# A four-layer convolution sequence on one core: layer 0 in two strips, layers 1 and 2 as sixteen tiles, and a new model of the order

## The chip, the core and the metric

The kernel runs on one core of one Trainium2 chip. TensorE (PE in the profile), VectorE (DVE), ScalarE (ACT), GpSimd (POOL) and the DMA queue of SyncE (SP) each run their own instruction stream in order and wait for each other by semaphores. PEld is TensorE's loading of weights. The metric is the device time of one execution in microseconds (us); the median of the kernel before is 5206.15 us over three runs (5203.51 to 5209.27). The profile is one further execution.

## The reference

A batch of 32 images of 56 x 56 positions and 96 channels, float32, passes through four layers. Cut to what is computed:

```python
# layer 0: router, expert mix, 1x1 up to 384, 3x3 depthwise, 1x1 down to 96, shortcut
pooled = jnp.mean(x, axis=(1, 2))
rw = jax.nn.sigmoid(pooled @ Wr + br)
Wk = jnp.einsum('be,ecm->bcm', rw, Wpw)
h = jnp.einsum('bhwc,bcm->bhwm', x, Wk) + (rw @ bpw)[:, None, None, :]
h = jax.nn.relu(_bn(h, g1, b1, m1, v1))
h = _cond_dw(h, Wdw, bdw, rw)              # 3x3 depthwise, mixed of 4 experts by rw
h = jax.nn.relu(_bn(h, g2, b2, m2, v2))
Wk2 = jnp.einsum('be,emf->bmf', rw, Wpwl)
h = jnp.einsum('bhwm,bmf->bhwf', h, Wk2) + (rw @ bpwl)[:, None, None, :]
x = _bn(h, g3, b3, m3, v3) + shortcut
# layer 1: x + 5x5 depthwise convolution
# layer 2: relu, 3x3 depthwise, 1x1 (96 to 96), batch norm
# layer 3: shifted window attention (7x7 windows, 3 heads) and an MLP (96, 384, 96), both with
#          layer norm and a residual
```

## The kernel before, in words

The image lies with its channels on the partitions (`xT`, 96 x 3136). Four stages work on four images at a time, one step apart (the loop at L1507): the router of layer 0 (`stage_router`), the rest of layer 0 (`stage_conditional`), layers 1 and 2 (`stage_depthwise`), and layer 3 (`stage_swin`).

**Layer 0.** `stage_conditional` takes the image in `NSTRIP` = 4 strips of `STRIP` = 14 rows, and in each of them `NB` = 3 blocks of 128 of the 384 channels. `expand` makes a block's rows, with a margin row above and below, by two matmuls `banks<-xT,wmix` and two ScalarE activations into `h1`. The nine taps of the 3x3 filter follow: the first on ScalarE (`h<-h,mix`), the other eight on VectorE (`h<-h,mix,h`, 784 elements). `relu` is on ScalarE. `project` brings a strip's 384 channels back to 96, by three matmuls `banks<-h,wmix` for each 7 rows; ScalarE scales and shifts the result into `y`, and GpSimd adds it to `xT` (`add`).

**Layers 1 and 2.** `stage_depthwise` does the 5x5 and the 3x3 depthwise filter on TensorE with banded weights. 8 channels x 4 rows (`RB`) are the 32 rows of a tile, 14 blocks of rows and 56 columns the moving side. `x1` is filled from `xT` by 12 DMAs (`x<-xT`, 32 x 14 x 56). A set is 12 products of 32 x 32 that run beside each other (`together`), one for each of 3 groups and 4 quarters; a filter of n columns needs 2n sets, as a band reaches into the next block of rows. Layer 1 has two halves of 10 sets with 392 columns, layer 2 two parts of 6 sets with 392 and 448. In the trace a product is two records. ScalarE evicts (`x<-banks`), DMAs bring the result back to rows (`filtered<-x`, 36 an image), and the matmuls `banks<-pw,filtered` do the 1x1 product.

**Layer 3.** Its residual rows `res` carry the mean in an extra column. In `perceptron` GpSimd first adds that column (`tb<-res`), then the bias (`tb<-tb,L_conv_b`), and VectorE adds the sum from the banks (`tb<-banks,tb`); a DMA writes `out`.

**What sets the order.** Every instruction is recorded with a target (`PLAN`, `interleave`) by `Recorder`, which then plays a model of the engines (`order`): whatever is ready on an engine and has its buffers starts, the earliest target first. The model's prices are `cost`, `COST`, `LANDING` (of a DMA), `CROSSING` and `TO_TENSOR` (from one engine's end to another's start), and `SHARING` (GpSimd and VectorE slow each other). Where TensorE has nothing for `SPARE_AFTER`, a spare matmul `banks<-ident` of 128 columns is put in. The instructions are then issued in the order found (`give`, L490, whose L500 is therefore the line of nearly every row of the profile). On the chip each engine keeps that order, and waits when an operand is late.

The lines that carry the steps of the change:

```python
    ("sync", "dma_start"): (550, 0),
...
            if e == "gpsimd" or e == "vector" and w.calls[0][0] == "scalar_tensor_tensor":
...
            y = chip.new(ys)
            chip.scalar.activation(y, pt[:C, :RT], AF.Identity, bias=bias3, scale=s3)
...
            chip.gpsimd.tensor_tensor(rows, y, rows, ALU.add)
```

Of the kernel before, what the change touches and what calls it, by code (L numbers as in the profile page):

```python
# [38 lines left out]
RB = 4  # L39
NBLK = H // RB  # L40
STRIP = 14
# [46 lines left out]
def banded(k, before, back):  # L88

    w = np.zeros((NQ, 8, RB, NG, 2, k.shape[2], 8, RB), np.float32)
    for q in range(NQ):
        for g in range(NG):
            first = 32 * g + 8 * ((q - g) % NQ if back else q)
            for m in range(2):
                for row in range(RB):
                    for r in range(RB):
                        dy = RB * m + row - r - before  # L100
                        if 0 <= dy < k.shape[1]:
                            for c in range(8):
                                w[q, c, row, g, m, :, c, r] = k[first + c, dy]
    return w.reshape(P, NG, 2 * k.shape[2], 32)
# [3 lines left out]
def tile_scores_in_range(ctx: ExitStack, tc: tile.TileContext, a: dict, flag: bass.AP):  # L108
# [38 lines left out]
    ("vector", "scalar_tensor_tensor"): (150, 1.16), ("vector", "tensor_tensor"): (180, 0.96),  # L147
    ("vector", "tensor_scalar"): (190, 0.78), ("vector", "tensor_reduce"): (180, 0.95),
    ("vector", "tensor_copy"): (180, 1.1), ("vector", "reciprocal"): (180, 6.2),
    ("scalar", "activation"): (200, 0.72), ("scalar", "copy"): (200, 0.72),  # L150
    ("gpsimd", "tensor_tensor"): (200, 2.1), ("gpsimd", "memset"): (150, 0),
    ("sync", "dma_start"): (550, 0),
}
LANDING = 3000
IMAGE_LANDING = 12000

PLAN = {"router": (-0.14, 1), "conditional": (0.72, 1.14), "depthwise": (1.48, 1.13), "swin": (3.09, 0.92)}
CROSSING = 350

TO_TENSOR = {"vector": 1500, "gpsimd": 1500, "scalar": 1000, "sync": 700}  # L160
SPARE_AFTER = 250
SHARING = 1.36


def cost(engine, method, args, kw):
    if method == "preload_act_table_set":
        return 1300
    out = kw["out"] if "out" in kw else args[0]
    n = math.prod(out.shape[1:])
    if engine == "tensor":  # L170
        if method == "transpose":
            return 127
        k, m = args[1].shape[0], math.prod(args[1].shape[1:])
        if k == 32 and m == 32:
            return 68 * n / 392
        if k == 32:
            return 86
        if m == 32:
            return 75 if n < 128 else 255
        return 195 if n < 128 else 80 + 1.6 * n  # L180
    if len(args) > 3 and args[3] == ALU.pow:
        return 200 + 200 * n
    fixed, each = COST[engine, method]
    if engine == "scalar":
        if kw.get("accum_out") is not None:
            fixed += 190
        if hasattr(kw.get("scale"), "shape"):
            each += 0.37 if hasattr(kw.get("bias"), "shape") else 0.23
        elif hasattr(kw.get("bias"), "shape"):
            each += 0.25  # L190
    return fixed + each * n
# [69 lines left out]
class Recorder:  # L261
# [77 lines left out]
    def order(self):  # L339
# [15 lines left out]
        for w in self.work:  # L355
            for b in w.uses:
                b.left = len(b.users)
        queues = {e: [] for e in self.ENGINES}
# [7 lines left out]
        def available(w):  # L366
            need = {}
# [6 lines left out]

        running = {}

        def share(now):

            nonlocal count
            rate = SHARING if len(running) > 1 else 1.0  # L380
            for r in running.values():
                r["left"] -= (now - r["since"]) / r["rate"]
                r["since"], r["rate"] = now, rate
                r["end"] = free[r["work"].engine] = now + max(r["left"], 0.0) * rate
                heapq.heappush(events, (r["end"], count, r))
                count += 1
# [19 lines left out]
        def begin(w):  # L406
# [9 lines left out]
            if e == "gpsimd" or e == "vector" and w.calls[0][0] == "scalar_tensor_tensor":  # L416
                running[e] = {"work": w, "left": w.ns, "since": now, "rate": 1.0}
                share(now)
                return
            free[e] = now + w.ns  # L420
            heapq.heappush(events, (free[e], count, None))
            heapq.heappush(events, (free[e] + w.landing, count + 1, w))
# [8 lines left out]
        while left:  # L431
            for e in self.ENGINES:
                if free[e] > now:
                    continue
                held = []
                while queues[e]:
                    item = heapq.heappop(queues[e])
                    w = self.work[item[1]]
                    if not available(w):
                        held.append(item)  # L440
                        continue
                    begin(w)
                    left -= 1
                    if e == "tensor":
                        spares, begun = 0, True
                    break
                else:
                    if e == "tensor" and begun and self.spare and now >= free[e] + SPARE_AFTER and self.spare[2].free:
# [5 lines left out]
                        w.ns = cost(e, "matmul", operands, {})  # L454
# [10 lines left out]
            while events and events[0][0] <= now:  # L465
                _, _, w = heapq.heappop(events)
                if isinstance(w, tuple):
                    put(w[0])
                elif isinstance(w, dict):

                    if w["end"] == now and running.get(w["work"].engine) is w:
                        del running[w["work"].engine]
                        w["work"].end = now
                        done(w["work"], now)
                        share(now)
                elif w is not None:
                    done(w, now)
# [26 lines left out]
def kernel(  # L504
# [17 lines left out]
    xTs = ring("xT", [C, H * W], 2)  # L522
    h2s = ring("h2", [P, NB, STRIP * W], 2)
    wmixs = ring("wmix", [C, M], 2)
    wmix2s = ring("wmix2", [P, NB * C], 2)
    ys = ring("y", [C, RT], 2)
# [9 lines left out]
    x3s = ring("x3", [P, NG, NBLK // 2 + 1, W], 1)  # L536
    oTs = ring("oT", [C + 1, 2 * RT], 2)
    x1s = ring("x1", [P, NG, NBLK + 1, W + 4], 1)
    x2s = ring("x2", [P, NG, NBLK + 2, W + 2], 1)
    filtereds = ring("filtered", [C + 1, H, W], 1)  # L540
    h1s = [ring(f"h1{k}", [P, STRIP + 2, W + 2], 1) for k in range(NB)]
    if general:
        ss = ring("scores", [PK, NP, PK], 6)
        pTs = ring("pT", [PK, RT], 4)
# [3 lines left out]
    nc.sync.dma_start(out=xTs.tiles[0], in_=x[0])  # L548


    rooms = [h2s.tiles[0].rearrange("p k n -> p (k n)"), x3s.tiles[0].rearrange("p g m w -> p (g m w)")]
# [94 lines left out]

    held = []
# [13 lines left out]
    band5 = later([P, NG, 10, 32], layouts["k5"], "band5")  # L661
    centre = hold(scratch(P, 64, 1).rearrange("p (n c) -> p n c", n=2), layouts["centre"])
    band3 = later([P, NG, 6, 32], layouts["k3"], "band3")
# [34 lines left out]
    def first_others():  # L698
# [9 lines left out]
        for t in x1s.tiles + x2s.tiles:  # L708
# [17 lines left out]
    def last_others():  # L726
        for g in range(NG):
            for n in range(2):
                at = 5 * n + 2
                nc.vector.tensor_tensor(band5[:, g, at], band5[:, g, at], centre[:, n], ALU.add)  # L730
# [15 lines left out]
    for h1 in h1s:  # L746
        nc.gpsimd.memset(h1.tiles[0], 0.0)
# [15 lines left out]
    def stage_router(b):  # L763

        xT = chip.new(xTs).part(*range(NROW))
# [14 lines left out]
        pooled_w = new_small("pooled_w", [C, P], 1)  # L780
# [21 lines left out]
        prod = new_small("prod", [P, NB * NM, E], 1)  # L802
# [19 lines left out]
        mixed[b] = xT, wmix, wmix2, mix, bias1, biasd, bias3  # L822
        yield 1

    def stage_conditional(b):

        xT, wmix, wmix2, mix, bias1, biasd, bias3 = mixed.pop(b)
        h1s_of = {}

        def expand(strip, k):  # L830

            h1s_of[strip, k] = chip.new(h1s[k]).part(0, 1)

            if strip in (0, NSTRIP - 1):
                chip.gpsimd.memset(h1s_of[strip, k][:, 0 if strip == 0 else STRIP + 1], 0.0)
# [3 lines left out]
            for half, n in enumerate(((last - first + 1) // 2, (last - first) // 2)):  # L839
# [9 lines left out]
                    h1s_of[strip, k][:, at : at + n, 1 : W + 1].part(half),  # L849
# [9 lines left out]
        def project(n, h2):  # L859

            pt = chip.new(mm)
            with chip.together():
                for q in range(NB):
# [3 lines left out]
                        h2[:, q, n % 2 * RT : (n % 2 + 1) * RT],  # L867
# [3 lines left out]
            y = chip.new(ys)  # L871
            chip.scalar.activation(y, pt[:C, :RT], AF.Identity, bias=bias3, scale=s3)
            return y

        def add(n, y):
            rows = xT[:, 7 * n * W : 7 * (n + 1) * W].part(n)
            chip.gpsimd.tensor_tensor(rows, y, rows, ALU.add)

        def projections(strip, h2):
            for n in (2 * strip, 2 * strip + 1):  # L880
# [11 lines left out]
        def relu(h2, k):  # L892
            part = h2[:, k].part(k)
            chip.scalar.activation(part, part, AF.Relu, bias=biasd[:, k : k + 1], scale=s2[:, k : k + 1])

        behind = iter(())
        filtered_before = None
        for at, (strip, k) in enumerate(blocks):
            if k == 0:
                h2 = chip.new(h2s).part(*range(NB))  # L900
            ahead = expand(*blocks[at + 1]) if at + 1 < len(blocks) else iter(())
            h1 = h1s_of[strip, k]
            acc = h2[:, k].part(k).rearrange("p (r w) -> p r w", w=W)
            for t in range(9):
# [7 lines left out]
                yield 1  # L912
                if t in (0, 3):
                    next(ahead, None)
                    yield 1
                if t == 4 and filtered_before:
                    relu(*filtered_before)
                if t in (6, 8):
                    next(behind, None)
                    yield 1  # L920
            filtered_before = h2, k
            if k == NB - 1:
                for _ in behind:
                    yield 1
                behind = projections(strip, h2)
# [5 lines left out]
        added[b] = xT  # L931

    def stage_depthwise(b, res):
# [3 lines left out]
        def lines(t):  # L937

            return t.rearrange("(c r) m w -> c r m w", r=RB)

        x1 = chip.new(x1s)
        x2 = chip.new(x2s).part(0, 1)
# [624 lines left out]
```

## Time and profile before

| | |
|---|---|
| median of three runs | 5206.15 us |
| span of the profiled execution | 5212.6 us |
| granted TensorE clock, mean | 0.985 |
| instructions in the profile | 139630 |
| DMA packets, share of 16 engines | 481940, 14.8% |
| HBM read, written | 41.60 MB, 38.54 MB |
| VectorE taps `h<-h,mix,h` | 3072, mean 1113 ns |
| GpSimd `xT<-y,xT` | 256, mean 1838 ns |
| `tb<-res`, `tb<-tb,L_conv_b` on GpSimd | 256 and 256 |
| DMAs `x<-xT`, `filtered<-x` | 384, 1152 |

A row of the profile's groups has the line, the engine, the operation, what is written from what is read, the shape, how often, the busy time, the mean of one in ns, and the idle time of the engine just before such instructions with what ended it. A row of the timeline has the start, the length and the instructions merged into it. A row of the windows has the stretch, its length, the busy time and number of instructions of PE, PEld, DVE, ACT and POOL, then the granted clock, the DMA engines' share and GB/s.

### The profile page before, as it was taken

The numbers are of one execution on the slowest core, as the hardware profiler recorded it, in microseconds if no ns is written. First come the engines' busy times: TensorE is split into PE (matmuls) and PEld (weight loads), VectorE is DVE, ScalarE is ACT, GpSimd is POOL, SyncE is SP. The second block draws the span as 40 slices with busy tenths as digits, with TensorE's granted clock in tenths as the row PEclk, the third lists the DMA queues.
The fourth block names the chain that finished last, engine by engine and source line by source line (L and its number), as shares of the span: only waits on it lengthen the run. The fifth ranks groups of instructions, "written<-read, shape, count | busy, mean of one in ns | idle before, by whom it ended". The sixth has DMA issues, their size and how long they took to land.

```text
span 5212.6 us, 139630 instructions
## 1 busy us (share of the span) xinstructions
PE 5050.6 (97%) x58578; PEld 3343.9 (64%) x58578; DVE 4300.9 (83%) x5561; ACT 3836.9 (74%) x7649; POOL 3028.8 (58%) x2432
## 2 busy tenths in 40 slices
PE   5789999999999999999999999999999999999999
PEld 4556666666666666666666666666666666666677
DVE  7877988888888888888888888888888888888722
ACT  3457778877778777777877777877777877777755
POOL 5455766565665556666555665656576555566533
PEclk9899999999999999999999999999999999999999
DMA  1111101111111111111111111111111111110110
GB/s 43 23 28 37 38 18 32 33 39 36 39 21 30 31 39 36 39 23 30 33 35 37 37 30 26 30 36 38 37 35 22 32 33 39 36 39 21 23 28 19
DMA packets 482577, 166.34 MB, mean 32 GB/s; under 512 B 477951, under 2 KB 478612, under 8 KB 478868
## 3 DMA queue, kind: packets, MB, share of 16 engines
q1 hardware_dynamic: 481940, 157.33, 14.8%
q8 instruction: 463, 7.59, 0.6%
q14 instruction: 174, 1.43, 0.1%
HBM read 41.60 MB, written 38.54 MB: 15 GB/s over the span
## 4 chain that ended last, share of the span: by engine, by line
PE 74%; POOL 10%; DVE 5%; ACT 5%; issue 4%; DMA 1%; SPq 0%; ACTq 0%; DVEq 0%; POOLq 0%
PE banks L500 74%; DVE h L500 3%; POOL tb L500 3%; POOL lnd L500 2%; POOL xT L500 2%; ACT exps L500 2%; POOL exps L500 2%; POOL var L500 1%; ACT hid L500 1%; ACT h L500 1%; DMA out<-tb 1%; DVE wmix L500 1%; DVE hid L500 1%; ACT slots L500 0%; DVE res L500 0%
## 5 line engine op out<-in xcount | busy, mean ns | idle before, releaser
L500 DVE SCALAR_TENSOR_TENSOR h<-h,mix,h 128x784 f32<-128x784 f32 x3072 | 3309.6, 1113 | 71.1 <-ACT h L500 54.0
L500 POOL TENSOR_TENSOR var<-var,mhalf 112x4 f32<-112x4 f32 (+1 forms) x512 | 775.2, 1519 | 426.3 <-DVE var L500 419.6
L500 PE MATMUL banks<-x,band 32*32 32x392 f32 x24576 | 856.3, 510 | 0.0
L500 POOL TENSOR_TENSOR xT<-y,xT 96x392 f32<-96x392 f32 x256 | 470.2, 1838 | 445.5 <-ACT y L500 444.1
L500 PE MATMUL banks<-xT,wmix 96*128 96x448 f32 (+1 forms) x1536 | 697.9, 553 | 0.5 <-DVE wmix L500 0.5
L500 ACT ACTIVATE h<-h,biasd,s 128x784 f32<-128x784 f32 x384 | 398.9, 1039 | 366.1 <-DVE h L500 366.0
L500 ACT ACTIVATE hid<-banks,c 128x448 f32<-128x448 f32 (+1 forms) x768 | 436.5, 582 | 288.3 <-PE banks L500 279.9
L500 POOL TENSOR_TENSOR tb<-res 112x384 f32<-112x384 f32 (+1 forms) x256 | 476.4, 1866 | 286.7 <-DMA out<-tb 196.7
L500 PEld LDWEIGHTS banks<-w,hid 128*112 128x112 f32 x5376 | 584.7, 183 | 82.0 <-issue 37.8
L500 PE MATMUL banks<-hT,w 96*128 96x448 f32 (+1 forms) x1536 | 615.6, 502 | 0.2 <-DVE tb L500 0.2
L500 POOL TENSOR_TENSOR lnd<-res,var 112x384 f32<-112x384 f32 (+1 forms) x512 | 594.8, 1168 | 32.8 <-PE banks L500 16.2
L500 ACT ACTIVATE h<-banks,bias,s 128x448 f32<-128x448 f32 (+1 forms) x768 | 538.6, 709 | 91.0 <-PE banks L500 85.4
L500 PE MATMUL banks<-w,hid 128*112 128x96 f32 x5376 | 593.1, 267 | 7.4 <-ACT hid L500 6.4
L500 PE MATMUL banks<-h,wmix 128*96 128x392 f32 x1536 | 557.7, 501 | 15.7 <-ACT h L500 15.7
L500 PEld LDWEIGHTS banks<-x,band 32*32 32x32 f32 x24576 | 404.7, 103 | 250.9 <-issue 165.9
L500 ACT ACTIVATE exps<-banks 49x196 f32<-49x196 f32 x1536 | 506.2, 330 | 40.2 <-PE banks L500 15.3
L500 POOL TENSOR_TENSOR exps<-exps,keep_column 49x147 f32<-49x147 f32 x224 | 207.1, 925 | 480.8 <-ACT exps L500 427.4
L500 PEld LDWEIGHTS banks<-h,wmix 128*96 128x96 f32 x1536 | 244.1, 165 | 256.8 <-issue 209.2
L500 PEld LDWEIGHTS banks<-xT,wmix 96*128 96x128 f32 x1536 | 261.2, 192 | 200.7 <-issue 95.5
L500 DVE TENSOR_REDUCE var<-lnsq 112x4 f32<-112x388 f32 (+1 forms) x512 | 253.1, 497 | 157.6 <-POOL lnd L500 118.1
L500 ACT ACTIVATE h<-h,mix 128x784 f32<-128x784 f32 x384 | 364.5, 949 | 18.0 <-POOL h L500 10.1
L500 PEld LDWEIGHTS banks<-hT,w 96*128 96x128 f32 x1536 | 256.4, 190 | 144.9 <-issue 74.8
(132 smaller groups left out, 7460.2 us busy)
## 6 DMA issues: line engine op xcount, KB each, us to landing
xT<-in_x SPq DMA_DIRECT2D x32, 1176.0 KB
x<-xT SPq DMA_DIRECT2D x384, 98.0 KB
out<-tb SPq DMA_DIRECT2D x128, 168.0 KB
filtered<-x SPq DMA_DIRECT2D x384, 49.0 KB
filtered<-x SPq DMA_DIRECT2D x384, 42.0 KB
out<-tb SPq DMA_DIRECT2D x128, 126.0 KB
filtered<-x SPq DMA_DIRECT2D x384, 7.0 KB
wpw<-in_L_conv_Wpw SPq DMA_DIRECT2D x1, 576.0 KB
```

The source lines that it names most:

```text
L500: getattr(getattr(self.nc, w.engine), method)(*args, **kw)
```

## The change

Layer 0 goes in two strips of 28 rows: a tap is 1568 elements, a block needs four `expand` matmuls, and the three blocks share two `h1` buffers and four `h2` buffers. The scale of the last batch norm goes into the weights `wpwl` once at the start; what is left of `y` is one VectorE instruction that adds the bank, `bias3` and `xT`. Layers 1 and 2 take 2 channels x 16 rows as a tile's 32 rows, of which 10 come out of both filters; six such pieces cover the 56 rows. A set has 16 products of 336 columns, and no band reaches over. An image is three parts (`NSET`) of 32 channels: for each 16 DMAs bring `x1` from `xT`, two DMAs from `nought` put zeros where the image ends, 11 DMAs go to `filtered`. The first filter of a part is one block of 80 products, the second one of 48. The MLP's extra column is added by VectorE, in one instruction for each 96 columns. The model gets new prices, prices TensorE by tiling, [...]and picks TensorE work of the tiling in use where targets are close.

```diff
-RB = 4
-NBLK = H // RB
-STRIP = 14
+NSET = 3
+NSLOT = NSET * NQ
+BIN, BMID, BOUT = 16, 12, 10
+NBLK = -(-H // BOUT)
+STRIP = 28
...
-    ("sync", "dma_start"): (550, 0),
+    ("sync", "dma_start"): (120, 0),
 }
+AHEAD = {"vector": 77, "scalar": 100, "gpsimd": 37, "tensor": 0, "sync": 0}
 LANDING = 3000
 IMAGE_LANDING = 12000
-PLAN = {"router": (-0.14, 1), "conditional": (0.72, 1.14), "depthwise": (1.48, 1.13), "swin": (3.09, 0.92)}
-CROSSING = 350
-TO_TENSOR = {"vector": 1500, "gpsimd": 1500, "scalar": 1000, "sync": 700}
-SPARE_AFTER = 250
-SHARING = 1.36
+PLAN = {"router": (-0.041, 1.15), "conditional": (0.667, 0.94), "depthwise": (1.583, 0.874), "swin": (3.095, 1.065)}
+CROSSING = 863
+TO_TENSOR = {"vector": 1428, "gpsimd": 3328, "scalar": 1321, "sync": 530}
+SPARE_AFTER = 286
+CHANGE = 170
+SAME = 0.0231
...
+            if w.in_memory:
+                begun_at = max(now, port[0])
+                port[0] = begun_at + ns
...
+                    if e == "tensor" and SAME:
+                        if first is None:
+                            first = item
+                        if item[0] > first[0] + SAME:
+                            held.append(item)
+                            w = None
+                        elif w.tiling != last[0]:
+                            held.append(item)
+                            continue
...
-            y = chip.new(ys)
-            chip.scalar.activation(y, pt[:C, :RT], AF.Identity, bias=bias3, scale=s3)
-            return y
+            return pt[:C, :RT]
         def add(n, y):
             rows = xT[:, 7 * n * W : 7 * (n + 1) * W].part(n)
-            chip.gpsimd.tensor_tensor(rows, y, rows, ALU.add)
+            chip.vector.scalar_tensor_tensor(rows, y, bias3, rows, ALU.add, ALU.add)
...
+        for u in range(NSET):
+            x1 = chip.new(x1s)
+            for r in range(BIN):
+                chip.sync.dma_start(
+                    out=lines(x1)[:, r].rearrange("c o m w -> c (o m) w")[:, :, 2 : 2 + W].part(r),
+                    in_=xT[32 * u : 32 * u + 32, r : r + BOUT * (NBLK - 1) + 1 : BOUT],
+                )
+            inputs.append(x1.part(*range(BIN)))
+            yield 2
+        def products(weights, src, u, dx, back):
+            banks = [chip.new(cv) for _ in range(NQ)]
+            with chip.together():
+                for d in range(dx):
+                    for o in range(NQ):
                         for q in range(NQ):
+                            come, go = (o, q) if back else (q, o)
+                            ks, os = slice(32 * come, 32 * come + 32), slice(32 * go, 32 * go + 32)
                             chip.tensor.matmul(
+                                banks[come][os, : NBLK * W].rearrange("p (m w) -> p m w", w=W),
+                                weights[ks, NQ * u + go, d],
+                                src[ks, go, :, d : d + W],
+                                start=(d == 0),
+                                stop=(d == dx - 1),
                             )
...
+            for m, r in ((0, 0), (NBLK - 1, H + 1 - BOUT * (NBLK - 1))):
+                chip.sync.dma_start(
+                    out=lines(x2)[:, r, :, m, 1 : 1 + W],
+                    in_=nought[:, None, :].to_broadcast([NQ * 2, NQ, W]),
+                )
...
+            wrapped = x3.rearrange("p o m w -> p (o m) w").part(*range(NQ))
+            chip.gpsimd.tensor_copy(wrapped[:, :, W:], wrapped[:, :, :3])
+            into = filtered[32 * u : 32 * u + 32].part(u)
+            for r in range(BOUT):
+                chip.sync.dma_start(
+                    out=into[:, 1 + r : 2 + r + BOUT * (NBLK - 1) : BOUT],
+                    in_=lines(x3)[:, r].rearrange("c o m w -> c (o m) w")[:, :, 3:],
+                )
...
+        for u in range(NSET):
+            waiting.append((u, first_filter(u)))
+            yield 6
+            if u > 0:
+                second_filter(*waiting.pop(0))
+                yield 4
...
-            chip.gpsimd.tensor_tensor(tb, src[:, :, :C], src[:, :, C:].to_broadcast([LT, n, C]), ALU.add)
-            chip.gpsimd.tensor_tensor(tb, tb, b2[:LT, None, :].to_broadcast([LT, n, C]), ALU.add)
+            chip.gpsimd.tensor_tensor(tb, src[:, :, :C], b2[:LT, None, :].to_broadcast([LT, n, C]), ALU.add)
...
-            total = tb.rearrange("p j c -> p (j c)")
-            chip.vector.tensor_tensor(total, pt[:LT, : n * C], total, ALU.add)
+            for j in range(n):
+                chip.vector.scalar_tensor_tensor(
+                    tb[:, j], pt[:LT, j * C : (j + 1) * C], src[:, j, C:], tb[:, j], ALU.add, ALU.add
+                )
...
-            stages.append((stage_conditional(b), 167, when("conditional", b)))
+            stages.append((stage_conditional(b), 195, when("conditional", b)))
```

## The prediction

> **What bounds the kernel now.** I read the busy shares and the chain that ended last, then one repeat of the steady state, then the groups with shapes kept apart, then the timelines of TensorE (PE) and of the DMA queue (SPq).
>
> ```profile
> PE 5050.6 (97%) x58578; PEld 3343.9 (64%) x58578; DVE 4300.9 (83%) x5561; ACT 3836.9 (74%) x7649; POOL 3028.8 (58%) x2432
> ...
> PE 74%; POOL 10%; DVE 5%; ACT 5%; issue 4%; DMA 1%; SPq 0%; ACTq 0%; DVEq 0%; POOLq 0%
> ```
>
> PE is busy nearly always and carries the chain. The rows repeat every 310.5 us, which is two images; a window of that length:
>
> ```profile
> 1310.50:1621.00 310.50, 306.52 (x3598) 200.40 (x3597) 269.59 (x345) 239.49 (x481) 185.66 (x151) 0.99 0.16 33
> ```
>
> So an image takes 155.2 us, PE is idle for 2 of them, VectorE for 20. 32 x 155.2 = 4968; the other 245 us of the span of 5212.6 are filling and draining. The median of the runs shown, 5206.15, is 6 us under the span; I subtract these 6 at the end.
>
> ```profile
> L500 PE MATMUL banks<-x,band 32*32 32x392 f32 x19968 | 653.1, 495 | 0.0
> L500 PE MATMUL banks<-x,band 32*32 32x448 f32 x4608 | 203.6, 574 | 0.0
> L500 PE MATMUL banks<-ident 128*128 128x128 f32 x1672 | 242.5, 288 | 39.9 <-ACT h L500 29.0 <-ACT y L500 10.0 <-ACT slots L500 0.4
> L500 DVE SCALAR_TENSOR_TENSOR h<-h,mix,h 128x784 f32<-128x784 f32 x3072 | 3309.6, 1113 | 71.1 <-ACT h L500 54.0 <-POOL h L500 2.0
> ```
>
> Busy times of PE overlap, so I count from each start to the next: band matmuls (layers 1 and 2) 824 us, spares (ident; two records each, 0.13 us a record) 215, everything else 4011; idle 153. Work without spares is thus 4835. How a band set (12 products, 24 records) behaves:
>
> ```profile
> 2511.61 14.20 PE L500 MATMUL banks<-x,band 32*32 32x392 f32 x480
> ...
> 2539.58 0.92 PE L500 MATMUL banks<-x,band 32*32 32x392 f32 x24
> 2540.43 3.58 PE L500 MATMUL banks<-pw,filtered 97*112 97x97 f32 x34
> ...
> 2630.60 1.77 PE L500 MATMUL banks<-x,band 32*32 32x448 f32 x24
> 2632.30 1.29 PE L500 MATMUL banks<-pw,filtered 97*112 97x97 f32 x8
> 2633.52 1.02 PE L500 MATMUL banks<-x,band 32*32 32x448 f32 x24
> 2634.47 0.83 PE L500 MATMUL banks<-pw,filtered 97*112 97x97 f32 x6
> ```
>
> Twenty sets in one block take 0.70 each (two waves of 0.33, which is 392 columns at 1.2 per ns); a lone set takes 0.85. The set at 2630.60 follows an idle PE of 2.7 us and takes 1.70 instead of 0.95. Last, what a load costs SPq:
>
> ```profile
> 1389.57 2.70 SPq L500 DMA_DIRECT2D x<-xT  x4
> ...
> 1420.30 4.76 SPq L500 DMA_DIRECT2D filtered<-x  x7
> ```
>
> Every SBUF-to-SBUF DMA, small or large, holds SPq for 0.6 us, and they follow each other at 0.67. The landing events lie 2.7 us behind the issue for x<-xT and 2.1 for filtered.
>
> [...] a last matmul before another tiling takes 0.09 us more (192 against 98 ns for pw,filtered). [...] Here twelve start 6.5 ns apart, 78 ns for a wave of 330; sixteen are not in this trace. [...]
>
> **Part by part.**
>
> Band matmuls. Their number stays (384 products an image), but they come as 24 sets of 16 and have 336 columns: waves of 336/1.2 = 0.28 us, a set 0.57. In the changed order they stand in blocks of 80 (five taps) or 48 (three): 189 blocks, where now there are 468. Edges of a block cost 0.19 (first wave 0.03 longer, drain 0.16). Per image 24 x 0.57 + 6 x 0.19 = 14.8 us, 474 in all: 350 less than 824. Entries into the tiling fall by 279 x 0.09 = 25 us; other changes of tiling rise by 75, 7 us. If sixteen tiles were bound by issue and each record took 330/12 = 27 ns, a set would take 0.88 and 240 us of this would be lost; the 6.5 ns between starts speak against it.
>
> Expansion of layer 0. Two strips compute 58 rows with their margins, four computed 62; the order has 192 matmuls of 448 columns and 576 of 392, now the other way round. At 0.415 and 0.355 us a record (two each) 614 becomes 568: 46 less. PE's work is then 4835 - 350 - 25 + 7 - 46 = 4421.
>
> Spares. The order has 968 instead of 836: 132 x 0.26 = 34 us more. They stand at 20 an image in the steady part (10 now), in a cluster ahead of the last four projections.
>
> VectorE. 1536 taps of 1568 elements replace 3072 of 784. Back to back the latter start 0.946 apart, and 392 elements (hid) 0.484: a slope of 1.18 ns, hence 1.87 for 1568; with half of the overhead saved by a longer row 1.82. 48 x 1.84 = 88, and about 8 of waiting for POOL, against 101 now. New: 8 sums xT from the banks at 0.49 (as oT<-hid,banks), 4 us, and 28 small sums tb at 0.16 to 0.25, 5 us instead of 3.4. In all 131 to 136 us an image against 134. It stays hidden while an image takes over 145.
>
> POOL loses the xT sums (14 us an image) and one of two tb passes (15). It was hidden[...]. ScalarE loses y (4.9 us) and half of the first-tap instructions, gains a little on wider copies: 5 less of 120. Both hide behind PE.
>
> DMAs. An image now has 12 loads x<-xT, then 48; 36 stores to filtered, then 33; and 6 new small ones from nought. At 0.67 SPq is held for 65 us of 155, so not its bound; packets rise from 15 to 19 thousand an image, from 15% to about 19% of the engines. What counts is latency. Sixteen loads must be issued between the last sum xT of an image and its first band block: the wait of the third load is for that last sum, so 13 spacings of 0.68 follow, and a landing of 2.35 (taken between the two measured). With the sum (0.55), its place in VectorE's queue (0.3) and two hand-overs of 0.1, the block can start 12.2 us after the last projection. In the changed PE order the work between the two, priced from the rows above, is 8.3, 9.0, 16.8 and 9.8 us in a pattern of four images: the queue waits 4.0, 3.2, 0 and 2.4. The second set of loads lands at 23.8, and its block stands such that 0, 5.0, 2.6 and 0.2 more are waited for. The first block of layer 2 needs the zeros from nought, which are in SPq behind all 48 loads, three stores and the next image's load, which itself waits for the landings; 49 spacings more or less, two landings and 2 us of the rest make 39.4: 0, 5.8, 5.7 and 11.0. Together 4.0, 14.0, 8.3, 13.6; over 32 images with their own positions 339 us. Now there is none of this: the trace has 45 us of other PE work between the last sum (1385.4) and the first band set (1429.9). Nothing hides a wait at the head of PE's queue, as all later matmuls stand behind it, and ScalarE's evictions behind those.
>
> Half of PE's present waits for other engines beyond the start (111 us, for lnd and h among them) should vanish behind these: -50.
>
> Sum: 5212.6 - 414 + 34 + 339 - 50 = 5122 us of span, 5115 as a median.
>
> **Rivals.**
>
> 1. The loads are no wait at all. If the new form issues like out<-tb (0.32 us), 13 spacings take 4.2 us, the block is ready at 7.5, and the gain stays whole: 5212 - 414 + 34 = 4832, some other waits make it 4850. For it: that one DMA of the queue is cheap. Against: three shapes of SBUF-to-SBUF DMA all show 0.6.
>
> 2. Slower: the same waits are larger. Price: each 0.1 us on an issue adds 1.3 us to the first and 4.8 us to the third of these times; a landing of 3.5 adds 1.2 to each[...]. The gain of 380 us is 11.9 us an image, so it decides from there, only 1.3 above my 10.6. With issues at 0.75 and 1.5 cold starts an image the waits are 16 us: about 5350 at the outer end, 5290 in the middle.
>
> 3. VectorE becomes the bound: 136 us and 12 of waiting for ScalarE and PE an image, 148 x 32 + 245 = 4980. For it: the cluster of spares before the last projections. Against: it has 20 us to spare while PE waits for loads.
>
> That the change does not do what it says is excluded by the changed order.
>
> **How the numbers follow.** Forecast 0.44, its own range 5020 to 5215; loads free 0.18; slower 0.33; VectorE 0.05. A measurement of this kernel can tell 0.2%, 10 us, from no change. Of the forecast 0.03 and of the slower case 0.03 lie within it. Faster: 0.41 + 0.18 + 0.05 = 0.64; same 0.06; slower 0.30. The range goes from the free loads to the middle of the slower case: 4850 to 5320.
>
> **What would show it.** Band matmuls at 450 to 500 us start to start, x band blocks of 160 and 96 records; PE waiting for DMA x<-xT and x<-nought some 10 us an image (in its waits and in the chain); SPq x<-xT at 0.6 each; taps at 1.85 to 1.95; VectorE under 90%. Wrong would be: waves of more than 0.35 us, loads issued in under 0.4, or PE waiting chiefly for VectorE.

## The result, and the profile after

The changed kernel takes 5375.76 us (median of 4 runs, 5366.86 to 5381.98) where the kernel before takes 5206.23. The ratio is 1.0325, 95% interval 1.031 to 1.0339: slower by 3.3%, where 5115 us was forecast. The profiled execution has a span of 5365.1 us.

The page's busy shares and its chain by engine, after:

```profile
PE 4917.6 (92%) x58844; PEld 3400.5 (63%) x58844; DVE 4100.7 (76%) x4918; ACT 3711.6 (69%) x7393; POOL 2413.2 (45%) x2022
...
PE 69%; SPq 12%; ACT 7%; DMA 5%; DVE 4%; issue 3%; POOL 0%; ACTq 0%; DVEq 0%
```

PE, VectorE, ScalarE and GpSimd are all busy for less time than before (PEld alone for a little more), and yet the span is longer. By these shares PE is without work for 447 us, 162 before. The chain shows where: the DMA queue and the landings, 1% before, now hold 17% of it. The repeat of the steady state is four images long; its window (start and end, length, then the busy time of PE, PEld, DVE, ACT and POOL with instruction counts, the granted clock, the DMA share and GB/s):

```profile
2164.10:2809.40 645.30, 600.57 (x7296) 411.93 (x7274) 511.35 (x609) 462.94 (x925) 305.09 (x249) 0.97 0.17 38
```

An image takes 161.3 us, 6.1 more than before. PE stands still for 11 of them (it was 2), and its granted clock is 0.97 (it was 0.99). The groups of the changed operations, shapes kept apart (count, busy us, mean ns, then the idle time ahead of them and what ended it):

```profile
L538 PE MATMUL banks<-x,band 32*32 32x336 f32 x24576 | 743.9, 519 | 295.4 <-DMA x<-nought 119.3 <-DMA x<-xT 109.5 <-issue 35.1
L538 PE MATMUL banks<-ident 128*128 128x128 f32 x1936 | 285.8, 288 | 33.3 <-ACT h L538 26.4 <-ACT hid L538 2.5 <-DVE xT L538 1.8
L538 DVE SCALAR_TENSOR_TENSOR h<-h,mix,h 128x1568 f32<-128x1568 f32 x1536 | 2909.4, 1903 | 166.0 <-ACT h L538 159.0 <-POOL var L538 1.6
L538 DVE SCALAR_TENSOR_TENSOR tb<-banks,res,tb 112x96 f32<-112x96 f32 x896 | 257.1, 309 | 505.5 <-PE banks L538 489.9 <-ACT h L538 11.7 <-ACT x L538 1.3
```

No band matmul waited before; now 295 us of idle PE lie ahead of them, most of it ended by the two transfers that the prediction named. Of the 35 us under issue, 33 are zeros too: they lie six times ahead of the first block of layer 2, which then starts 0.09 us after its zeros have landed; where the profile names x<-nought it is 0.04 to 0.14 us. The zeros thus hold up PE for 152 us, the loads for 110. VectorE waits for PE (tb), not the other way round. What such a wait does is seen in PE's timeline (start, length, operation, and in brackets the idle time before it):

```profile
910.10 6.19 PE L538 MATMUL banks<-x,band 32*32 32x336 f32 x160 [4.10 <-DMA x<-xT]
...
931.11 4.09 PE L538 MATMUL banks<-x,band 32*32 32x336 f32 x160
...
1089.78 0.76 PE L538 MATMUL banks<-hT,w 96*128 96x336 f32 x2
1103.04 3.77 PE L538 MATMUL banks<-x,band 32*32 32x336 f32 x96 [12.51 <-DMA x<-nought]
```

The first two blocks hold the same 160 records. The one that follows 4.1 us of idle PE takes 6.19 us, the one without a wait 4.09. The last block waits 12.5 us for zeros, and the queue of that time shows why:

```profile
1081.79 11.54 SPq L538 DMA_DIRECT2D x<-xT  x16
1093.38 0.64 SPq L538 DMA_DIRECT2D filtered<-x  x1
1094.12 0.61 SPq L538 DMA_DIRECT2D x<-nought  x1
1095.16 0.35 SPq L538 DMA_DIRECT2D xT<-in_x  x1
1095.56 0.66 SPq L538 DMA_DIRECT2D filtered<-x  x1
1096.27 0.60 SPq L538 DMA_DIRECT2D x<-nought  x1
```

Sixteen loads stand ahead of the first zeros and hold SPq for 11.5 us. The second store of zeros is issued 1.1 us after the load of a whole image (1176 KB), and by the landing events it lands 6.7 us after its issue, the first one 1.8. Over the run, the 84 stores of zeros that were issued within 6 us of an image load land after a median of 6.6 us, the other 108 after 1.8. The trace of before has the same: 189 stores to filtered within 6 us of an image load land after 6.2 us, the other 963 after 2.1.

The same sum as in the prediction, start to start, in us:

| term | forecast | measured |
|---|---|---|
| band matmuls | 474 | 731 |
| other work of PE, spares apart | 3947 | 3926 |
| spares | 249 | 260 |
| PE idle (153 - 50 + 339) | 442 | 439 |

The sum of the waits came out as forecast. The miss is in the first line, 257 us, of which the other three give back 13.

### The profile page after: what moved, and what is told of

The parts are those of the page before. It is cut to its first block, busy times and chain, and to the rows that moved or that the text cites. A ratio compares the mean times of both kernels' runs of the same rounds, so it can differ in the third digit from the quotient of the medians.

```text
span 5365.1 us, 140457 instructions
## 1 busy us (share of the span) xinstructions
PE 4917.6 (92%) x58844; PEld 3400.5 (63%) x58844; DVE 4100.7 (76%) x4918; ACT 3711.6 (69%) x7393; POOL 2413.2 (45%) x2022
## 4 chain that ended last, share of the span: by engine, by line
PE 69%; SPq 12%; ACT 7%; DMA 5%; DVE 4%; issue 3%; POOL 0%; ACTq 0%; DVEq 0%
PE banks L538 69%; SPq L538 12%; DVE h L538 3%; ACT h L538 2%; DMA x<-nought 2%; ACT exps L538 2%; DMA x<-xT 1%; ACT hid L538 1%; ACT slots L538 1%; DMA xT<-in_x 1%; ACT xT L538 0%; DVE xT L538 0%; DMA filtered<-x 0%; ACT qT L538 0%; ACT v L538 0%
## 5 line engine op out<-in xcount | busy, mean ns | idle before, releaser
L538 DVE SCALAR_TENSOR_TENSOR h<-h,mix,h 128x1568 f32<-128x1568 f32 x1536 | 2909.4, 1903 | 166.0 <-ACT h L538 159.0
L538 PE MATMUL banks<-x,band 32*32 32x336 f32 x24576 | 743.9, 519 | 295.4 <-DMA x<-nought 119.3
L538 PEld LDWEIGHTS banks<-x,band 32*32 32x32 f32 x24576 | 439.8, 111 | 562.3 <-issue 342.2
L538 POOL TENSOR_TENSOR tb<-res,L_conv_b 112x384 f32<-112x384 f32 (+1 forms) x256 | 504.9, 1980 | 314.0 <-DMA out<-tb 168.4
L538 DVE SCALAR_TENSOR_TENSOR tb<-banks,res,tb 112x96 f32<-112x96 f32 x896 | 257.1, 309 | 505.5 <-PE banks L538 489.9
L538 PE MATMUL banks<-xT,wmix 96*128 96x392 f32 (+1 forms) x1536 | 631.1, 517 | 12.0 <-DVE wmix L538 11.4
L538 ACT ACTIVATE h<-banks,bias,s 128x392 f32<-128x392 f32 (+1 forms) x768 | 515.3, 692 | 52.7 <-PE banks L538 47.2
L538 POOL TENSOR_TENSOR exps<-exps,keep_column 49x147 f32<-49x147 f32 x224 | 252.7, 1128 | 600.5 <-ACT exps L538 470.0
L538 ACT ACTIVATE x<-banks 128x336 f32<-128x336 f32 x384 | 146.0, 456 | 342.7 <-PE banks L538 342.7
L538 ACT COPY x<-banks 128x336 f32<-128x336 f32 x384 | 142.1, 456 | 273.3 <-PE banks L538 244.4
```

Of the source, the lines that this page charges most:

```text
L538: getattr(getattr(self.nc, w.engine), method)(*args, **kw)
```

## The experiments

The theory with which I began: W, loads and zeros that arrive late stop PE at the head of its queue, as the order was planned with a DMA price of 120 ns where the trace has 613 on average (550 in the plan before). Its rival B: the band sets themselves are slower than forecast, waits or not.

### The order's DMA price

```
-    ("sync", "dma_start"): (120, 0),
+    ("sync", "dma_start"): (620, 0),
```

> The changed kernel, but its order is planned with a DMA price of 620 ns on SyncE's queue, not 120; the work is the same. Theory W (waits for x<-xT and x<-nought at the head of TensorE's queue, because the order takes loads for five times cheaper than they are): the planner puts other matmuls ahead of the band blocks, TensorE's idle time falls from 439 us to under 300, and the time from 5376 to 5150-5250. Rival B (the loss lies in the band sets themselves, which take 0.75 us for 0.57): idle time may fall, but the time stays above 5300.

Measured: 5120.18 us, ratio to before 0.9834 (0.9817 to 0.985). The chain of its page:

```profile
PE 79%; ACT 12%; DVE 6%; issue 2%; POOL 0%; SPq 0%; DMA 0%; ACTq 0%; DVEq 0%; POOLq 0%
```

Its waits of PE (us in all, number, longest):

```profile
PE banks L538 <- DMA x<-xT: 9.2, 4, 3.4
```

DMA and its queue are gone from the chain. Waits of matmuls for x<-xT fall from 109.5 to 9.2 us, idle PE falls from 439 to 199, band matmuls from 731 to 645. With one number of the planner a loss of 3.3% becomes a gain of 1.7%. What it moved can be measured, as means over the 32 images: from the last projection of an image to its first band block the changed kernel has 13.7 us, 3.9 of them idle; this one 18.6 us, 1.0 idle. My step had 12.2 us as the earliest start, and half of the changed kernel's blocks do start no more than 12.3 us after it, the earliest at 11.5. W holds so far. But the whole order moved with the price, so the next runs keep the order.

The waits for zeros do not vanish, though the profile names none: 39 us of idle PE, 152 before, still lie ahead of the first blocks of layer 2, under issue and ACT. One of these blocks, and the queue before it:

```profile
1527.94 4.24 PE L538 MATMUL banks<-x,band 32*32 32x336 f32 x96 [3.61 <-issue]
...
1520.26 0.35 SPq L538 DMA_DIRECT2D xT<-in_x  x1
1520.66 1.28 SPq L538 DMA_DIRECT2D x<-nought  x2
```

In this order the queue issues the stores of two parts in turn, so the block needs the first of these two, behind the image load. By the landing events it lands at 1527.85, and the block starts 0.09 us later. All 21 blocks that wait here start 0.09 to 0.12 us after such a landing.

### The waits taken away, in an unchanged order

The order is planned as in the changed kernel, and the named transfers are then not issued.

```
                 chip.sync.dma_start(
                     out=lines(x2)[:, r, :, m, 1 : 1 + W],
                     in_=nought[:, None, :].to_broadcast([NQ * 2, NQ, W]),
+                    left_out=True,
```

> The changed kernel in exactly its order, with the six small stores of zeros into x2 left out (the rows beyond the image keep what the eviction wrote). Theory W: TensorE's waits for x<-nought (119 us in front of matmuls, up to 48 more in front of weight loads) go, and with them the half clock after each: 100 to 190 us less, 5185-5275. Rival: another late DMA (the loads of the next set) ends the same waits, and under 60 us are won.

Measured: 5221.09 us, 155 less than the changed kernel. That is in W's span. The waits of PE show that the loads still stop it:

```profile
PE banks L541 <- DMA x<-xT: 100.2, 24, 8.5
PE banks L541 <- DMA filtered<-x: 68.5, 25, 6.6
```

The second run leaves out the loads of x1 too.

> The changed kernel in exactly its order, with the stores of zeros and all 48 loads of x1 an image left out (the band matmuls run on zeros). Theory W with the sum of the trace: TensorE's idle time falls from 439 to about 150 us, the half clock of the band blocks goes too (band 731 to about 620): 290 + 110 less, 4950-5030. If the waits were not what the time hangs on (VectorE or ScalarE ending next): above 5200.

Measured: 4897.39 us, 478 less than the changed kernel and beyond what I expected. Its page:

```profile
PE 4784.0 (98%) x58844; PEld 3331.3 (68%) x58844; DVE 4098.8 (84%) x4918; ACT 3702.6 (76%) x7393; POOL 2469.5 (50%) x2022
```

Its band group:

```profile
L541 PE MATMUL banks<-x,band 32*32 32x336 f32 x24576 | 646.0, 453 | 6.2 <-issue 6.2
```

Idle PE is 101 us, 338 less; the waits for filtered<-x, whose stores remain, are gone too. Band matmuls take 633 us start to start, 98 less though they are the same instructions in the same order: that is the price of the half clock behind the waits. In the clock records of the traces 225 us of band work lie at half clock in the changed kernel, 4 us here. Other matmuls take 35 us less. The first band block now starts 9.5 us after the last projection, as early as the order allows. What is left is that 633 us are still not 474, and there are no waits to blame.

### Why a set takes longer

In a block of five sets the waves last as follows (ns, taken from the starts in the trace, from each sixteenth or twelfth to the next, the last one to the next matmul of another kind; warm is full clock, cold is half). The first two are the changed kernel's blocks at 931.11 and 910.10, the third is the block at 882.78 of the run with twelve products below:

```
changed, 16 products, warm   307 282 427 310 454 310 447 312 445 728    sum 4.02 us
changed, 16 products, cold   530 560 560 560 708 559 764 560 611 708    sum 6.12 us
12 of the 16 products        307 282 295 293 286 286 285 287 282 806    sum 3.41 us
```

The granted clock of the cold block is half from 908.2 to 915.1, so its last waves are at full clock again. Forecast was 280 for each, and 0.19 us for the edges of a block. First idea: neighbours share a row or a column of the array.

```
-                            come, go = (o, q) if back else (q, o)
+                            come, go = ((q + o) % NQ, q) if back else (q, (q + o) % NQ)
```

> The changed kernel, but the 16 products of a set follow each other along the diagonals of the 4 x 4 grid of tiles, no two neighbours in one row or column of the array; order of all else the same. Theory B1 (the 0.19 us pause in each set comes from neighbours that share rows or columns): sets go from 0.75 to about 0.58 us, band matmuls from 731 to about 580 us, the time to 5230-5280. Theory B2 (it comes with sixteen tiles whatever their order): 5376 within 15 us, sets at 0.75.

Measured: 5375.25 us. The band group is unchanged:

```profile
L538 PE MATMUL banks<-x,band 32*32 32x336 f32 x24576 | 748.0, 520 | 300.1 <-DMA x<-nought 119.6 <-DMA x<-xT 106.2 <-issue 38.0
```

So it isn't the order in the set, as far as one other order can show it. Next, the number, at the better DMA price:

```
                                 stop=(d == dx - 1),
+                                left_out=o == NQ - 1,
```

> The order planned with a DMA price of 620 ns (5120 us), with the last four products of each set of 16 left out at the same places (a quarter of the band products is not computed). Warm sets of 16 take 0.80 us in a block of five, edges included, where 0.61 was forecast. Theory I (a set costs one pause of 0.19 us and 17 ns a product, and this must fit into its two waves of 0.28): with twelve it fits, sets take 0.57 us, blocks of 160 records 3.1 us instead of 4.02 in their new length of 120 records, band matmuls fall from 645 to about 500 us, time 4960-5040. Theory S (short waves of 336 columns have the pause whatever their number): blocks stay at 4.0, band over 620, time within 20 us of 5120.

Measured: 5125.79 us. A block of five in PE's timeline:

```profile
882.78 3.48 PE L541 MATMUL banks<-x,band 32*32 32x336 f32 x120
```

The band group:

```profile
L541 PE MATMUL banks<-x,band 32*32 32x336 f32 x18432 | 589.6, 468 | 79.9 <-issue 51.3 <-DMA x<-xT 11.6 <-ACT h L541 8.4
```

On the sets theory I holds: with twelve products every inner wave takes 282 to 295 ns, with sixteen every second one 427 to 454. The twelve that are left use three of the four columns of tiles (in the second filter, rows), so this run does not tell their number from their place. The cause of the pause is not shown. With it, sixteen bring nothing over twelve: 0.38 us a wave for 0.286. The edge of a block is the second error: the last wave takes 0.4 to 0.5 us more than those before it, with twelve products as with sixteen.

On the time theory I is wrong: 69 us of band work were saved and nothing came of it. The order is that of the run with 620, so the two traces can be set side by side. Idle PE rises from 199 to 230 us, and 27 us of this lie ahead of the first blocks of layer 2: 66 us for 39, in 26 images for 21, each of them 0.09 us after its zeros have landed. In 12 of these waits a spell of half clock begins (in 4 before), the mean clock falls from 0.982 to 0.969, and the other matmuls take 44 us more. Shorter sets bring PE to the zeros earlier, and the zeros do not come as much earlier.

### The parts that I had costed at nothing

```
-            chip.gpsimd.tensor_tensor(tb, src[:, :, :C], b2[:LT, None, :].to_broadcast([LT, n, C]), ALU.add)
+            chip.gpsimd.tensor_tensor(tb, src[:, :, :C], src[:, :, C:].to_broadcast([LT, n, C]), ALU.add)
+            chip.gpsimd.tensor_tensor(tb, tb, b2[:LT, None, :].to_broadcast([LT, n, C]), ALU.add)
...
+            chip.vector.tensor_tensor(total, pt[:LT, : n * C], total, ALU.add)
```

> The order planned with a DMA price of 620 ns, with the sums of tb made as before the change (two GpSimd passes and one VectorE addition of 384 elements, instead of one pass and up to four small VectorE sums). My step said that this part is hidden either way: within 20 us of 5120. Rival: GpSimd's second pass (15 us an image) and its contention with VectorE come back, 50 us or more slower.

Measured: 5128.48 us, 8 from 5120 and within the 20. As far as one number tells, this part is hidden either way. The rival's two costs are in the trace of before: the pass `tb<-res` is 478 us, 15 an image, and GpSimd's `xT<-y,xT` takes 1007 ns in the median where VectorE is busy for less than a tenth of it (50 of them), 1505 where it is for nine tenths or more (188). It is not the price of the sums alone: the order was made anew for this run, and in it the zeros hold up PE for 56 us instead of 39. (The move of the xT sums was not tried alone.)

### Zeros without a transfer

```
-                chip.sync.dma_start(
-                    out=lines(x2)[:, r, :, m, 1 : 1 + W],
-                    in_=nought[:, None, :].to_broadcast([NQ * 2, NQ, W]),
-                )
+            edges = x2[:, :, 0 : NBLK : NBLK - 1, 1 : 1 + W]
+            chip.vector.tensor_tensor(
+                edges, edges, inside[:, None, :, None].to_broadcast([P, NQ, 2, W]), ALU.mult
+            )
```

> The order planned with a DMA price of 620 ns, and the six stores of zeros an image replaced by three multiplications of VectorE (448 elements a row, 0.6 us each) by a mask of rows. If loads and stores are hidden once the order knows their price: within 20 us of 5120. If the zeros' path (issue, landing, place behind the loads) still costs: 40 to 100 us less. VectorE gains 2 us an image; were it the bound, 60 us more.

Measured: 5041.92 us, ratio 0.9688 (0.9672 to 0.9704): 78 less. (The 0.6 us of a multiplication was an estimate; VectorE takes 0.55 us for 392 elements a row, `oT<-hid,banks` in the trace of before.) The 39 us of waits for zeros that the profile had put under other names are gone, idle PE falls from 199 to 150 us, and the other matmuls take 39 us less, with the clock at 0.987 instead of 0.982. So the stores still cost by their landing behind the image load; as the order was made anew, not all of the 78 us need be theirs.

> The changed kernel with its own DMA price of 120 ns, and the zeros by VectorE's mask in place of the six stores: the fourth corner of price (120, 620) and zeros (stores, mask); the others are 5376, 5120 and 5042 us. If price and zeros are two separate losses: the waits for x<-xT stay at about 100 us, 5180-5240, near the 5221 of the run that left the stores out. If the price acted only through the zeros (the stores are planned far too early behind 48 loads): below 5100.

Measured: 5201.06 us, ratio 0.9988 (0.9977 to 0.9998), PE waiting 104 us for x<-xT. Price and zeros are two losses: the mask is worth 175 us at a price of 120 and 78 at 620; the price is worth 256 with the stores and 159 with the mask. They overlap: together they are worth 334, not 431.

### The price alone, in the kernel before

```
-    ("sync", "dma_start"): (550, 0),
+    ("sync", "dma_start"): (120, 0),
```

> The kernel before, with nothing but its planner's DMA price changed from 550 to 120 ns. If the price is wrong for every form of this kernel: TensorE waits for x<-xT and filtered there too, 50 us or more slower than 5206. If it does harm only since the change, which has less other work between the last sum of layer 0 and the first band block: within 30 us of 5206.

Measured: 5899.31 us, ratio 1.1325 (1.1269 to 1.138). Neither of my two cases: slower by 692 us, and not by waiting for transfers. The largest line of PE's waits:

```profile
PE banks L500 <- POOL lnd L500: 343.9, 95, 13.7
```

PE waits for GpSimd's normalised rows, 51 us before. Of the 692 us, 354 are idle PE, 255 go to other matmuls, with the clock at 0.934 instead of 0.985, and 88 to more spares. The price moves far more in the order than the loads. How it comes to lnd was not followed up; this stays open.

### Spares

```
-SPARE_AFTER = 286
+SPARE_AFTER = 2500
```

> The order planned with a DMA price of 620 ns (5120 us, 2447 records of spare matmuls that occupy TensorE for 324 us), and spares put in only after 2.5 us of idle TensorE in the model, not 0.286. Theory P (the spares stand on the path: the chip does not have the idle time that the model sees): 150 to 250 us less, 4870-4970. Rival (they fill real waits for ScalarE and VectorE, and keep the clock up): 5120 or more, idle time up by what the spares lose, band blocks at half clock more often.

Measured: 5150.15 us. Spares fall from 324 to 44 us, idle PE rises from 199 to 332, the clock falls to 0.948. With a wait of 0.9 us, and the mask:

> The 5042 us kernel (DMA price 620, mask) with spares put in after 0.9 us of idle TensorE in the model instead of 0.286. With 97% busy and 150 us idle, if a part of its 2389 spare records (327 us) stands where the chip has no idle time: 30 to 80 us less. Rival, as the run with 2.5 us: idle time and half clock eat it up, 5042 or more.

Measured: 4953.64 us, ratio 0.9522 (0.9506 to 0.9537), the fastest of all, 4.8% under the kernel before. In a window of its steady part (columns as above) PE is busy for 97.8% at full clock:

```profile
1310.00:1610.00 300.00, 293.42 (x3748) 201.49 (x3747) 267.47 (x316) 231.01 (x466) 150.30 (x124) 1.00 0.19 42
```

The same threshold with the stores of zeros:

> The order planned with a DMA price of 620 ns, the six stores of zeros as in the change, and spares after 0.9 us of idle TensorE in the model (with 0.286: 5120 us; with 2.5: 5150; with the mask and 0.9: 4954). If the gain of the mask run came from the threshold alone: 5030 within 25 us (5120 less the same 88). If the stores need the cover that spares give, as the waits for loads did: 5090 or more.

Measured: 5113.92 us, only 6 under 5120, with 275 us idle and a clock of 0.964 (225 us and 0.986 with the mask). The second case. The profile puts PE's waits there under ScalarE and issue, but 59 us of them are zeros again: in 24 images the first block of layer 2 starts 0.09 us after their landing. The clock says more. The clock records of before and of the changed kernel hold full and half clock and nothing between (162 and 493 us at half); if it is so in these runs too, their mean clocks give an estimate of the time at half: 368 us here for 184 with a threshold of 0.286, and with the mask 138 for 131. Without the stores the spares can go and the clock stays; with them it does not. Only some 34 of the 368 us begin in a wait for zeros, so what sets off the rest is not settled.

## Why the prediction was wrong

**Bound.** PE's work carries the time, and VectorE stays hidden: right. VectorE's taps start 1.84 us apart with all waiting for GpSimd in it (in busy time 1843 ns with no GpSimd work beside them, 1903 on average), where I had put 8 us an image on top (in the trace of before a tap takes 1026 ns with no GpSimd work beside it and 1113 on average, 96 taps an image); its small sums 0.236; it is busy for 128 us an image, forecast 131 to 136.

**Waits.** Right in place: a load holds SPq for 613 ns, the first set lets the block start some 12 us after the last projection, and the two runs without transfers show that these waits are on the path. That the sum is right, 439 us idle for 442, is luck: loads and zeros stop PE for 262 us where I had 339, the stores to filtered for 51 where I had nothing, and the rest is 126 for 103. What I had not seen is what an image load ahead in the queue does to a small store: 4.8 us more to its landing. The trace of before had it, in 189 of its stores to filtered.

**The step that failed** is "Per image 24 x 0.57 + 6 x 0.19 = 14.8 us, 474 in all". It measured 731 us, in three parts:

- A set of 16 at 0.57. I took two waves of 0.28 because twelve products start 6.5 ns apart in the trace of before, and put the other case aside. Every second wave takes some 430 to 450 ns, beyond the 0.35 us that I had named as a sign of being wrong. Against the run with twelve products a warm block of five is 0.61 us longer and one of three 0.20 (2.46 against 2.26): 96 x 0.81 = 78 us.
- An edge at 0.19. I took it from lone sets. In longer blocks the last wave takes 0.4 to 0.5 us more, and this was in the trace of before: in its blocks of three sets the waves last 359, 333, 332, 328, 340 and 853 ns. The line at 2511.61 has it as well: from its start to the next matmul are 14.13 us, where 40 waves of 0.333 and an edge of 0.19 make 13.5. Why the edge grows with the block stays open. With the twelve products, 3.41 - 3.04 and 2.26 - 1.90 are 0.37 and 0.36 us too much: 96 x 0.73 = 70 us.
- Sets at full clock. The rest, 731 - 622 = 109 us, is half clock behind the waits; with the waits gone 98 us of it go. Rival 2 had such cold starts, 1.5 an image, but I had given the forecast none of them, though it had waits of up to 11 us in it. How long a wait must be, the traces do not tell exactly: in the trace of before the set at 2630.60 came at half clock (waves of 0.75 and 0.95 us, for 0.40 and 0.55 in the set at 2633.52) after a wait of 2.74 us, and in the changed kernel blocks that waited 2.95 and 2.99 us ran partly at half clock, others that waited 2.98 and 3.07 us did not. Every block that waited 3.1 us or longer did.

The cheaper expansion and the spares came out close enough: other work 3926 for 3947, spares 260 for 249.

**Rivals.** The slower case had the right consequence (half clock) and the wrong cause: issues stayed at 0.61 to 0.63. Its point of decision, waits above 11.9 us an image, assumed the whole gain in the band; with the band gain at 93 instead of 350 us the change loses already at 3.8. The case of free loads is what the run without transfers shows: 4897 for a forecast 4850. That the two are so near is luck again, as its band matmuls take 633 us and not 474; less idle time and less other work make up for most of it.

What the single terms are worth in the changed kernel is only shown for the waits and their half clock (478 us together). The pause and the edges are shown as durations, and their causes are open; the twelve-product run says that shortening a set need not shorten the kernel while a transfer stands behind it.

## What to carry to other kernels

A queue in program order is only as good as the prices it was planned with: compare each price of a planner with the duration in the trace first, above all of what is issued in long rows (48 loads at 120 instead of 613 ns). Where the profile puts a wait under issue or under an engine that had long been done, compare the start with the landings of the transfers that the instruction needs. When a wait at the head of TensorE's queue is expected, price the matmuls behind it at half clock too (here 109 of the 731 us of band matmuls). Take the duration of a packed set from blocks of the same length and number of tiles, and where the trace has none, carry the slower value in the forecast and not only in the range.

## What was not expected of the hardware

- Sixteen 32x32 products side by side take 0.38 us a wave on average, warm, at 336 columns, where twelve take 0.286: a third more work in a third more time. Sixteen bring nothing over twelve at this width.
- A small store of 7 KB lands after 6.6 us instead of 1.8 when an image load of 1176 KB has just been issued on the same queue (before the change, stores to filtered after 6.2 instead of 2.1).
- Half clock can follow 2.7 us of idle TensorE (before, the set at 2630.60), and stay away after 3.07 us (the changed kernel, the block at 3657.66).
- Fewer spare matmuls can cost or win: 280 us of them removed made the kernel 30 us slower in one order, 208 us removed made it 88 us faster in another.
